# Wider 0/1 comparisons and long-lived PSUM pools in a three-layer graph network on one core

## The chip, the cores and the metric

The kernel runs on one core of a Trainium2 chip. The metric is the time of one execution on the device, in microseconds (us). The core has five engines that run side by side: TensorE (PE, matrix products), VectorE (DVE), ScalarE (ACT), GpSimd (POOL) and SyncE (SP, which issues transfers). Products land in PSUM, which has eight banks; everything else is kept in SBUF.

## The reference

There are 2500 nodes with 256 features each and 80000 edges, sorted by their end node. The features are normalized and rectified, three graph layers follow, and a last product with residual makes the output:

```
m = concat([x[dst], x[src] - x[dst]]) @ W + b     # one row for each edge
s = segment_sum(m, dst);  cnt = segment_sum(1, dst)
h' = relu(s / max(cnt, 1))                        # three times, W0 b0, W1 b1, W2 b2
out = x + concat([h, h1, h2, h3]) @ Wf + bf       # h = max(layernorm(x), 0)
```

## The kernel before

The work on edges is done with a matrix A of counts: A[source, end] is how many edges run from one node to the other. A layer is then a product of A with the node features times a weight, plus each node's own part. A has 20 tiles of 128 source rows. Its columns, the end nodes, are cut into 417 stretches of 6 end nodes; 84 stretches are a group of 504 columns, and there are five groups, the last with 81 stretches.

**How A is built.** For each stretch the at most 256 edges that end in it are fetched (two indirect transfers by POOL for each block of 128 stretches, names `ed` and `es`) and turned into two small keys for each edge: the source's place within its tile (`key_m`), and the source's tile together with the end node's place within the stretch (`key_n`). `compare(b)` takes four stretches (a *window*, number b, of 105; 21 for each group) and makes 0/1 matrices on VectorE by comparing the keys with a ramp: `one_m` (4 x 2 x 128 columns) and `one_n` (4 x 120 and 4 x 80 columns). These are three instructions, `is_equal` on bf16. `counts(b)` multiplies one by the other on PE (eight products into one PSUM bank), and `take_counts(b, a)` copies the counts on ACT into `a`, the group's part of A. The 0/1 tiles have `AHEAD` = 4 buffers, and `compare` is called four windows ahead of `counts`.

**The head.** For the first group all this stands in one order written out by hand, in which each letter is a step with its index: B is `compare`, C is `counts`, E is `take_counts`; N normalizes two node tiles (on POOL from the third pair on), T transposes them on PE, R rectifies them, Z and F are products with weights (into `pz` banks), H and L split Z's result into a high and a low part (`zh` on ACT, `zl` on DVE); "sc" makes the scales of N on DVE; "ge" issues the two indirect transfers of a block of stretches, "ka" and "kb" compute key parts on DVE, "km" one on ACT, "kt" transposes the parts on PE. Each engine keeps the order in which its instructions are written. A part of that order, in the words of the string:

```
C2 B3 k21 Z9 k11 N8 L6 B4 E2 L5 C3 B5 C4 T8 E3 E4 C5 V9 R8 E5 ge3 ka2 H9 sc2 Z7 H7 F8 G7 B6 N3 N2 ka3 km2 T2 R2 km3
kb2 C6 T3 kb3 B7 L7 kt2 Z2 B8 B9 L9 E6 C7 k22 k12 kt3 H2 N4 E7 B10 k13 k23 Z8 L2 C8 T4 C9 E8
```

**Layer 0.** While PE multiplies group g of A with `zh` and `zl` (function `layer`, line 843), the next group is built between the products (`build`, line 811): in turns of three windows, `counts` of three, `take_counts` of three, then `compare` of the three windows four further on. Each group is also written to DRAM (`a_dram`), from where layers 1 and 2 read it.

**PSUM.** In layer 0, `ps_left` (four banks) holds the sums of the layer, `ps_right` (four banks) the counts. After layer 0 both pools are closed and two new ones opened: `ps_six` for the node products and the sums of pairs of groups, `ps_two` for the group without a partner (class `Alone`), which sums over the whole first half of a layer. `bank()` takes from `ps_six`; `any_bank()`, for the 14 sums of a layer's second half, takes six, then two from `ps_two`, and so on.

**Layers 1 and 2.** First the node features are multiplied with the weights in three rounded parts (class `Nodes`, ten pairs of tiles, two banks each); two pairs behind runs the lone group's product. Then come the two pairs of groups, seven sums each (class `Stream`), and after layer 2 the last product with `Wf`, ten pairs of tiles.

Of the kernel before, what the change touches and what calls it, by code (L numbers as in the profile page):

```python
# [8 lines left out]
F32 = mybir.dt.float32  # L9
# [3 lines left out]
PSUM = bass.MemoryType.PSUM  # L13
# [255 lines left out]
BF16 = mybir.dt.bfloat16  # L269
# [44 lines left out]
def by_windows(ctx: ExitStack, tc: tile.TileContext, x, src, dst, Ws, bs, Wf, bf, out, missing):  # L314
# [3 lines left out]
    P = 128  # L318
# [6 lines left out]
    DC = D // P  # L325
    R = E // P
    W = 6
    CH = 2
# [7 lines left out]
    NB = NT * W  # L336
    N1 = NT * (W - SKIP)
    BW = 4
    TURN = 3
    REP = 2  # L340
    AHEAD = 4
# [23 lines left out]
    hot = first_layer.enter_context(tc.tile_pool(name="hot", bufs=2))  # L365
# [6 lines left out]
    def bank():  # L372
        return ps[-1].tile([P, 512], F32, name="bank")
# [66 lines left out]
    def load_wb(l, queue=SP):  # L440
        raws[l] = wpool.tile([P, DC, 2, D], F32, name="wbf", bufs=1)
        ws[l] = wpool.tile([P, DC, D], F32, name="wt"), raws[l][:, :, 0, :]
        queue.dma_start(ws[l][1], Ws[l][D:2 * D, :].rearrange("(c p) d -> p c d", p=P))

    def load_wt(l, queue=SP):
        queue.dma_start(ws[l][0], Ws[l][0:D, :].rearrange("(c p) d -> p c d", p=P))

    def load_wf(l, queue=SP):
        if l == L:
            raws[l] = wpool.tile([P, DC, 2, D], F32, name="wbf", bufs=1)  # L450
        wfs[l] = raws[l][:, :, 1, :]
        queue.dma_start(wfs[l], Wf[l * D:(l + 1) * D, :].rearrange("(c p) d -> p c d", p=P))
# [22 lines left out]
    def load_b(l, queue=SP):  # L475
        queue.dma_start(brow[PAD:PAD + 1, l % 2, :], bs[l].rearrange("(o d) -> o d", o=1))
# [71 lines left out]
    def find_next():  # L548

        ahead.append(warmed(bank()))  # L550
        PEo.matmul(ahead[0][:, 0:1], shift[:, 1:], first, start=True, stop=True)
# [212 lines left out]
    def group_of(g):  # L764
        return sum(GWS[:g]) * W, GWS[g] * W
# [8 lines left out]
    windows = [(g, s, min(BW, GWS[g] - s)) for g in range(NG) for s in range(0, GWS[g], BW)]  # L774
    ones_of = {}

    def compare(b):
        if b >= len(windows):
            return
        g, s, nb = windows[b]  # L780
        w0 = sum(GWS[:g]) + s
        one_m = hot.tile([P, BW * CH, P], BF16, name="one_m", bufs=AHEAD)
        one_n = hot.tile([P, BW, NB + N1], BF16, name="one_n", bufs=AHEAD)
        for one, iota, keys_ in (
                (one_m[:, :nb * CH, :], iota_m, key_m[:, w0:w0 + nb, :, :].rearrange("p w j r -> p (w j) r")),
                (one_n[:, :nb, :NB], iota_n, key_n[:, w0:w0 + nb, 0, :]),
                (one_n[:, :nb, NB:], iota_n[:, NB - N1:], key_n[:, w0:w0 + nb, 1, :])):
            to = one.rearrange("p k (m r) -> p k m r", r=REP)
            DVEo.tensor_tensor(
                to, iota.rearrange("p (m r) -> p m r", r=REP).unsqueeze(1).to_broadcast(list(to.shape)),  # L790
                keys_.unsqueeze(2).to_broadcast(list(to.shape)), op=OP.is_equal)
        ones_of[b] = one_m, one_n

    counted = {}

    def counts(b):
        _, s, nb = windows[b]
        one_m, one_n = ones_of.pop(b)
        pb = counted[b] = bank()
        for w in range(nb):  # L800
            PEo.matmul(pb[:, w * NB:(w + 1) * NB], one_m[:, w * CH, :], one_n[:, w, :NB], start=True, stop=False)
            PEo.matmul(pb[:, (w + 1) * NB - N1:(w + 1) * NB], one_m[:, w * CH + 1, :], one_n[:, w, NB:],
                       start=False, stop=True)
# [108 lines left out]
    banks_of = ctx.enter_context(ExitStack())  # L912
    ps_left = banks_of.enter_context(tc.tile_pool(name="ps_left", bufs=4, space=PSUM))
    head[0].close()
    ps_right = banks_of.enter_context(tc.tile_pool(name="ps_right", bufs=4, space=PSUM))
# [26 lines left out]
    def flat(l):  # L942
        return raws[l].rearrange("p c t d -> p c (t d)") if l < L else wfs[l]

    class Split:

        def __init__(self, q, parts):
            h = hT[:, :, 2 * q * P:(2 * q + 2) * P]
            high, low, across = self.parts = [p.rearrange("p (c n) -> p c n", c=DC) for p in parts]
            ACTo.activation(high, h, AF.Copy, scale=DOWN)  # L950
            DVEo.tensor_sub(low, h, high.bitcast(F32))
            DVEo.scalar_tensor_tensor(across, low.bitcast(F32), -E12, high.bitcast(F32), op0=OP.mult, op1=OP.add)
            splits[q] = self
# [77 lines left out]
        extra = chain(degrees(g + 2) if g + 2 < WG else ())  # L1031
    first_layer.close()

    banks_of.close()
    ps_six = ctx.enter_context(tc.tile_pool(name="ps_six", bufs=6, space=PSUM))
    ps_two = ctx.enter_context(tc.tile_pool(name="ps_two", bufs=2, space=PSUM))
    turn_of = [0]

    def bank():
        return ps_six.tile([P, 512], F32, name="bank")  # L1040

    def any_bank():
        turn_of[0] += 1
        return (ps_six if (turn_of[0] - 1) % 8 < 6 else ps_two).tile([P, 512], F32, name="bank")

    tmps = ctx.enter_context(tc.tile_pool(name="tmps", bufs=6))
    stage = ctx.enter_context(tc.tile_pool(name="stage", bufs=4))
# [14 lines left out]
    def combine(to, x):  # L1062
        DVEo.tensor_sub(to[:, M3:S5 + 1, :], x[:, 1::2, :], x[:, 0:2, :])
        DVEo.tensor_sub(to[:, S2, :], to[:, M3, :], x[:, 3, :])
        DVEo.tensor_add(to[:, M4, :], to[:, S2, :], x[:, 2, :])
# [139 lines left out]
    class Alone:  # L1205

        def __init__(self, l, order):
            self.l, self.order = l, order
            self.c0, self.n = group_of(alone)
            self.to = [ps_two.tile([P, 512], F32, name="bank")[:, :self.n] for _ in range(DC)]  # L1210
            self.blocks = {}

        def make(self, p):
# [25 lines left out]
    def load_alone(k, order):  # L1239
        c = order[2 * k] // 2  # L1240
        st = stage.tile([P, 8 * GS], BF16, name="staged").rearrange("p (t n) -> p t n", n=GS)[:, :4, :]
        SPo.dma_start(st, a_dram[alone][:, 4 * c:4 * c + 4, :])
        loaded[k] = st
# [45 lines left out]
    def split(q):  # L1289
        tile_ = stage.tile([P, 4 * GS], F32R, name="staged")  # L1290
        Split(q, [tile_[:, k * 2 * D:(k + 1) * 2 * D] for k in range(3)])

    for l in range(1, L):
        order = orders[l]
        lone = Alone(l, order)
        if l == 1:
            load_alone(0, order)
            split(order[2])
        pending = []
        stream = Stream(l)  # L1300
        for i in range(Q + LAG):
            if 0 < i <= Q:
                lone.make(i - 1)
            if i < Q:
                q = order[i]
                n = Nodes(l, q)
                n.multiply(splits.pop(q), coming[0])
                if i + AHEAD_H < Q and i % 2 == 1:
                    load_alone((i + 1) // 2, order)
                n.parts()  # L1310
                n.combine()
                if i + AHEAD_H < Q and order[i + AHEAD_H] not in splits:
                    split(order[i + AHEAD_H])
                pending.append(n)
            if i and pending:
                pending.pop(0).sums()
            if 0 < i <= DC:
                lone.own(i - 1, 0)
            if i >= LAG:
                lone.multiply(i - LAG)  # L1320
            if i == Q - 1:
                load_alone(Q // 2 - 1, order)
                stream.load(3)
        stream.make(2)
        lone.end()
        turn_of[0] = 0
        if l + 1 < L:
            load_b(l + 1, SPo)
            load_wb(l + 1, SPo)
            load_wt(l + 1, SPo)  # L1330
        load_wf(l + 1, SPo)
        after = orders[l + 1]

        def tick(n):
            if n == 3:
                combine(wsum, ws[l][0].rearrange("p c (o n) -> p (c o) n", o=2))
            if n == 40 and l + 1 < L:
                DVEo.tensor_sub(ws[l + 1][0], ws[l + 1][0], ws[l + 1][1])
            if n in (49, 56):
                split(after[(n - 49) // 7])  # L1340
            if n == 63 and l + 1 < L:
                load_alone(0, after)
            if n in ((65,) if l + 1 < L else (63, 65)):
                split(after[2 + (65 - n) // 2])
            if n == 64:
                raw = flat(l + 1)
                coming[:] = [Forms(raw, [raw[:, c, :] if l + 1 < L else raws[L][:, c, 0, :] for c in range(DC)])]
                coming[0].high()
                coming[0].low()
            if n == 66:  # L1350
                coming[0].across()
            if n == 67:
                coming[0].last()

        stream.run(tick)

    order = orders[L]
    for i, q in enumerate(order):
# [9 lines left out]
        for k in range(2):  # L1368
            t = 2 * q + k
            add_to_acc(t, po[k])  # L1370
            n = P if t < NT - 1 else LAST
# [42 lines left out]
```

## Time and profile before

| | us |
|---|---|
| median of 3 runs (lowest to highest) | 480.16 (479.96 to 481.01) |
| the profiled execution, its whole time | 480.26 |
| its span, first to last instruction | 478.5 |
| PE busy | 468.4 |
| DVE busy | 386.2 |
| ACT busy | 302.5 |
| POOL busy | 43.1 |
| first product of layer 0 starts | 62.07 |
| last ACT work of layer 0 ends | 206.54 |
| final products under way | 458.8 |

The granted clock of TensorE was 0.996 of full speed. Busy time is what the profiler records for an engine's own instructions; neighbouring instructions of one engine can overlap in the records, so that busy times are read together with the distance from one start to the next. All operations are recorded by one helper at line 282, so that groups are told apart by their tile names and shapes and not by their lines. A few matmul records are missing from the trace.

### The profile page before, as it was taken

Reading aid. Unit: us, or ns where it says so; the run is one execution under the profiler, and the core shown is the slowest. Engines: PE = TensorE matmul, PEld = TensorE weight load, DVE = VectorE, ACT = ScalarE, POOL = GpSimd, SP = SyncE. Lnnn points to the kernel's source line nnn. Section 1 sums busy time; section 2 is a strip of 40 time slices with the busy share of each in tenths; the row PEclk is TensorE's granted clock in tenths of the full one; section 3 lists DMA queues with packets and bytes.
Section 4 is the critical chain, followed back from the end, with each engine's and each line's share of the span. In section 5 each row is a group of like instructions: output and inputs, shape, how many; then the busy total and the mean of one; then the engine's idle time right before and its main releaser. Section 6 shows DMA issues by size and latency. Waiting matters only on the chain.

```text
span 478.5 us, 7510 instructions
## 1 busy us (share of the span) xinstructions
PE 468.4 (98%) x2728; PEld 367.8 (77%) x2728; DVE 386.2 (81%) x836; ACT 302.5 (63%) x528; POOL 43.1 (9%) x66
## 2 busy tenths in 40 slices
PE   8999999999999999999999999999999999999994
PEld 4888888777877778868887877876788788688693
DVE  8999988988899884649987847877899687569785
ACT  5776577664654335067778866874787797497530
POOL 3683015200100001000000000000000000000000
PEclk9999999999999999999999999999999999999998
DMA  8310078990550905521258641110213955220033
GB/s 284 112 54 1 2 158 160 194 210 8 108 110 2 208 9 107 112 88 49 80 194 306 216 173 25 63 43 1 86 44 92 359 176 175 86 88 0 1 106 116
DMA packets 21847, 52.75 MB, mean 110 GB/s; under 512 B 1977, under 2 KB 12170, under 8 KB 21770
## 3 DMA queue, kind: packets, MB, share of 16 engines
q1 hardware_dynamic: 14730, 34.31, 21.2%
q0 software_dynamic: 5856, 16.51, 18.1%
q10 hardware_dynamic: 1216, 1.37, 0.9%
q8 instruction: 23, 0.38, 0.3%
q14 instruction: 22, 0.18, 0.1%
HBM read 36.72 MB, written 16.10 MB: 110 GB/s over the span
## 4 chain that ended last, share of the span: by engine, by line
PE 90%; DVE 4%; POOL 3%; ACT 1%; issue 1%; DVEq 0%; POOLq 0%; ACTq 0%
PE bank L282 87%; PE pz L282 3%; POOL acc L282 2%; DVE acc L282 1%; DVE staged L282 1%; POOL ed L282 1%; ACT junk L282 1%; POOL es L282 1%; DVE st L282 0%; DVE one_m L282 0%; ACT hT L282 0%; PE turned L282 0%; DVE zl L282 0%; DVE one_n L282 0%; DVE mv L282 0%
## 5 line engine op out<-in xcount | busy, mean ns | idle before, releaser
L282 ACT CAST block<-staged 128x1008 fp32r<-128x1008 bf16 x120 | 117.9, 1032 | 16.7 <-DVE staged L282 6.3
L282 ACT CAST a<-bank 128x480 fp32r<-128x480 f32 (+1 forms) x105 | 52.9, 566 | 60.2 <-PE bank L282 60.2
L282 PE MATMUL bank<-a,zh 128*128 128x504 f32 (+1 forms) x200 | 84.3, 422 | 0.0
L282 PE MATMUL bank<-block,zh 128*128 128x504 f32 (+1 forms) x200 | 83.7, 419 | 0.0
L282 DVE TENSOR_TENSOR one_m<-iota_m,key_m 128x1024 bf16<-128x1024 bf16 (+1 forms) x105 | 72.1, 686 | 14.1 <-PE bank L282 14.0
L282 PE MATMUL bank<-a,zl 128*128 128x504 f32 (+1 forms) x200 | 77.9, 389 | 0.0
L282 PE MATMUL bank<-block,zl 128*128 128x504 f32 (+1 forms) x200 | 77.3, 387 | 0.0
L282 PE MATMUL bank<-block,sh 128*128 128x504 f32 x160 | 69.0, 431 | 0.0
L282 DVE TENSOR_TENSOR one_n<-iota_n,key_n 128x480 bf16<-128x480 bf16 (+1 forms) x210 | 66.9, 360 | 0.0
L282 PE MATMUL bank<-block,staged 128*128 128x512 f32 (+1 forms) x312 | 66.5, 364 | 0.3 <-DVE staged L282 0.3
L282 PE MATMUL bank<-block,sl 128*128 128x504 f32 x160 | 62.6, 391 | 0.0
L282 PEld LDWEIGHTS bank<-block,staged 128*128 128x128 f32 x312 | 52.5, 188 | 10.8 <-DVE staged L282 0.5
L282 DVE TENSOR_TENSOR block<-staged 128x1008 fp32r<-128x1008 bf16 x40 | 47.0, 1205 | 5.2 <-PE bank L282 3.9
L282 PEld LDWEIGHTS <-one_m 128*128 128x128 bf16 x834 | 39.3, 98 | 10.4 <-issue 3.2
L282 PEld LDWEIGHTS bank<-a,zh 128*128 128x128 f32 x200 | 37.8, 189 | 10.7 <-issue 2.6
L282 PEld LDWEIGHTS bank<-block,zh 128*128 128x128 f32 x200 | 37.6, 188 | 10.8 <-issue 2.5
L282 PEld LDWEIGHTS bank<-block,zl 128*128 128x128 f32 x200 | 37.6, 188 | 10.6 <-issue 3.2
L282 PE MATMUL bank<-one_n,one_m 128*128 128x120 bf16 x834 | 44.9, 208 | 0.3 <-DVE one_n L282 0.2
L282 PEld LDWEIGHTS bank<-a,zl 128*128 128x128 f32 x200 | 37.7, 189 | 9.0 <-issue 2.6
L282 DVE TENSOR_TENSOR staged<-staged 128x1008 bf16<-128x1008 bf16 x40 | 27.2, 679 | 17.5 <-ACT block L282 17.1
L282 PE MATMUL pz<-wbf,hT 128*128 128x256 f32 x160 | 38.4, 385 | 0.1
L282 PEld LDWEIGHTS bank<-block,sh 128*128 128x128 f32 x160 | 30.1, 188 | 10.4 <-issue 3.5
(154 smaller groups left out, 597.3 us busy)
## 6 DMA issues: line engine op xcount, KB each, us to landing
staged<-a_dram SPq DMA_DIRECT2D x52, 504.0 KB, 4.0
a_dram<-a POOLq DMA_DIRECT2D x20, 630.0 KB, 9.0
out_dram<-acc SPq DMA_DIRECT2D x17, 128.0 KB, 1.8
acc<-in_x_dram POOLq DMA_DIRECT2D x3, 640.0 KB, 12.3
wbf<-in_L_gnn_Wf_dram SPq DMA_DIRECT2D x4, 256.0 KB, 7.2
acc<-in_x_dram SPq DMA_DIRECT2D x1, 896.0 KB, 9.5
acc<-in_x_dram ACTq DMA_DIRECT2D x1, 768.0 KB, 7.0
wbf<-in_L_gnn_W_dram SPq DMA_DIRECT2D x3, 256.0 KB
```

Source lines behind the costliest of these rows:

```text
L282: return self.tc.keep_in_program_order(call(*args, **kwargs))
```

## The change

The first edit lets `compare(b)` make the 0/1 matrices of two windows, b and b+1, in the same three instructions with twice the elements, if both are of the same group and b is not 0; the call for the second window then returns at once. The tiles are twice as large and have three buffers and not four. The calls stay where they were, in the hand order and in `build`.

The second edit keeps `ps_left` and `ps_right` open after layer 0. `bank()` now takes four banks from `ps_right`, then two from `ps_left`, in a ring of six; `any_bank()` takes four and four, in a ring of eight; the lone group takes its two banks from `ps_left`. Each ring has a counter of its own, and only that of `any_bank()` is set back at the end of a first half.

```diff
     def compare(b):
-        if b >= len(windows):
+        if b >= len(windows) or b in ones_of:
             return
         g, s, nb = windows[b]
         w0 = sum(GWS[:g]) + s
-        one_m = hot.tile([P, BW * CH, P], BF16, name="one_m", bufs=AHEAD)
-        one_n = hot.tile([P, BW, NB + N1], BF16, name="one_n", bufs=AHEAD)
+        two = b > 0 and b + 1 < len(windows) and windows[b + 1][0] == g
+        nb += windows[b + 1][2] if two else 0
+        one_m = hot.tile([P, 2 * BW * CH, P], BF16, name="one_m", bufs=3)
+        one_n = hot.tile([P, 2 * BW, NB + N1], BF16, name="one_n", bufs=3)
...
         ones_of[b] = one_m, one_n
+        if two:
+            ones_of[b + 1] = one_m[:, BW * CH:, :], one_n[:, BW:, :]
...
-        one_m, one_n = ones_of.pop(b)
+        one_m, one_n = ones_of[b]
...
-    banks_of.close()
-    ps_six = ctx.enter_context(tc.tile_pool(name="ps_six", bufs=6, space=PSUM))
-    ps_two = ctx.enter_context(tc.tile_pool(name="ps_two", bufs=2, space=PSUM))
-    turn_of = [0]
+    turn_of = [0, 0]
+
+    def next_bank(i, n):
+        turn_of[i] += 1
+        return (ps_right if (turn_of[i] - 1) % n < 4 else ps_left).tile([P, 512], F32, name="bank")
 
     def bank():
-        return ps_six.tile([P, 512], F32, name="bank")
+        return next_bank(0, 6)
 
     def any_bank():
-        turn_of[0] += 1
-        return (ps_six if (turn_of[0] - 1) % 8 < 6 else ps_two).tile([P, 512], F32, name="bank")
+        return next_bank(1, 8)
...
-            self.to = [ps_two.tile([P, 512], F32, name="bank")[:, :self.n] for _ in range(DC)]
+            self.to = [ps_left.tile([P, 512], F32, name="bank")[:, :self.n] for _ in range(DC)]
...
-        turn_of[0] = 0
+        turn_of[1] = 0
```

## The prediction

> **What bounds the kernel now.** I read the page's busy shares first, then the chain that ended last in order of time, then the stretches of the timeline where the two edits lie. First the page's engine row, then the pieces of the chain at the end of the first layer:
>
> ```profile
> PE 468.4 (98%) x2728; PEld 367.8 (77%) x2728; DVE 386.2 (81%) x836; ACT 302.5 (63%) x528; POOL 43.1 (9%) x66
> ```
>
> ```profile
> 62.42 143.51 PE bank L282 x1170
> 205.93 0.02 issue
> 205.96 0.58 ACT hT L282
> 206.54 0.04 issue
> 206.58 257.35 PE bank L282 x1088
> ```
>
> TensorE is the chain: from 62.42 to 463.94 us it leaves PE once, for ACT at 205.96. VectorE is at 81% and on the chain for 4% only, so time taken off VectorE counts only where TensorE waits for it. Before 62 us the chain does wander: through DVE, then POOL from 23.23 to 37.99, then PE, with DVE comparisons from 45.68 to 47.84. So there are two places to cost: the head (20 to 62 us) and the seam at 206 us.
>
> **Part 1: comparisons of eight stretches.** Windows pair up as (1,2), (3,4) and so on; each of the five groups has 21, so window 0 and the last of groups 1 to 4 stay single. That is 50 pairs, and 105 x 3 comparisons become 55 x 3: 150 VectorE instructions less, the elements unchanged. Groups by form, then the timeline inside layer 0:
>
> ```profile
> L282 DVE TENSOR_TENSOR one_m<-iota_m,key_m 128x1024 bf16<-128x1024 bf16 x104 | 71.8, 690 | 14.1 <-PE bank L282 14.0
> ...
> L282 DVE TENSOR_TENSOR one_n<-iota_n,key_n 128x480 bf16<-128x480 bf16 x104 | 41.7, 401 | 0.0
> ...
> L282 DVE TENSOR_TENSOR one_n<-iota_n,key_n 128x320 bf16<-128x320 bf16 x104 | 33.5, 322 | 0.0
> ```
>
> ```profile
> 115.16 0.69 DVE L282 TENSOR_TENSOR one_m<-iota_m,key_m 128x1024 bf16<-128x1024 bf16 x1
> ...
> 115.76 0.64 DVE L282 TENSOR_TENSOR one_n<-iota_n,key_n 128x480 bf16<-128x480 bf16 x2
> ...
> 116.32 0.68 DVE L282 TENSOR_TENSOR one_m<-iota_m,key_m 128x1024 bf16<-128x1024 bf16 x1
> ...
> 117.26 1.08 PEld L282 LDWEIGHTS <-one_m 128*128 128x128 bf16 x24 [0.27 <-DVE one_m L282]
> ```
>
> From the three means, an element costs (690-322)/704 = 0.523 ns and an instruction about 155 ns on top. The Trainium skill, "VectorE: DVE Perf Modes", section on the fixed extra latency per instruction, says the same (measured fixed term about 150 cycles; 1224 ns for a 2048-element bf16 tensor_tensor), and that would free 150 x 0.155 = 23 us. But starts count, not busy times: a window's three take 116.32-115.16 = 1.16 us from start to start, and 1824 elements x 0.523 = 0.954, so an instruction really costs (1.16-0.954)/3 = 0.07 us. The pair takes 2.32-0.21 = 2.11 us and VectorE is freed of 150 x 0.07 = 10.5 us. The trace's spacing decides.
>
> In layer 0 (62 to 183 us) even that is worth nothing: the row at 117.26 loads windows whose comparisons were done by 116.4 (the second) and 117.56 (the third, first loaded 16 loads later, at about 117.95). Its 0.27 is no stall; the matmul before began at 117.03, the next at 117.27, the normal spacing of 0.23. The pair runs one window further ahead with buffers for six, not four, so the cover grows. If it were gone, each turn's 1.2 us of loads would be exposed; nothing moves it there.
>
> In the head PE's stalls, as spacing above the normal of its form, are few: 0.56 us at 33 us (window 5), 0.63 before 38.03, 0.15 at 45.2 (window 10), 0.37 at 48 (window 12), 0.17 at 53.3 (window 16). Two of their rows, and between them the VectorE row that step (c) turns on:
>
> ```profile
> 33.07 0.69 PE L282 MATMUL bank<-one_n,one_m 128*128 128x120 bf16 x8 [0.23 <-DVE one_n L282]
> ...
> 36.05 0.33 DVE L282 TENSOR_SCALAR lo_i<-es 128x256 int32<-128x256 int32 x1 [0.23 <-DMA es<-longer,start_i]
> ...
> 38.03 0.44 PE L282 MATMUL turned<-shift,acc 128*128 128x128 f32 x2 [0.25 <-POOL acc L282]
> ```
>
> The hand order keeps its names; the call for the second window of a pair now does nothing, so its work moves up past what stood between.
> (a) Window 5 now waits for 5 and 6 together: +0.95 (2.11-1.16), less 0.21 each for pairs (1,2) and (3,4): stall +0.5. Queued behind it on DVE: the scale `sc2`, which POOL's normalizing (row at 34.76 below) waits for.
> (b) That normalizing then meets no comparison (window 6 stood there): 1.32 falls to about 0.55, so although it starts 0.5 late, the 0.63 stall at 38.03 shrinks by about 0.5. PE is even.
> (c) The last gather (`es`) is POOL's, and DVE stands at 36.05 for its landing; key parts and pair (7,8) queue behind it, and PE's key transposes and window 7 behind those. What delays POOL's earlier work delays this. POOL's rows:
>
> ```profile
> 15.68 0.55 POOL L282 TENSOR_SCALAR acc<-acc,rs,off 128x256 f32<-128x256 f32 x1 [2.04 <-DVE off L282]
> ...
> 24.05 1.36 POOL L282 TENSOR_SCALAR acc<-acc,rs,off 128x256 f32<-128x256 f32 x1
> ...
> 28.10 1.46 POOL L282 TENSOR_SCALAR acc<-acc,rs,off 128x256 f32<-128x256 f32 x1
> ...
> 34.76 1.32 POOL L282 TENSOR_SCALAR acc<-acc,rs,off 128x256 f32<-128x256 f32 x1 [1.23 <-DVE off L282]
> ```
>
> Alone 0.55 us; beside comparisons 1.32 to 1.46, that is, 0.8 to 0.9 of waiting, as long as the DVE instruction in progress and the next two. The skill speaks against this change here: "SBUF — State Buffer", section "Who interferes with whom", says a VectorE instruction with two SBUF inputs and a GpSimd one that reads SBUF share a port under a lock held for a whole instruction, and infers that descriptor writing for DMAs is spared. By the page a wait grows by one longer instruction, 1.22-0.69 = 0.53: with two normalizings (24.05, 28.10) ahead of the gather, 1.1 us. By the trace it grows by a whole triple, 0.95: 1.9 us, and more if gathers wait too (the two at 30.32 and 32.09 last 1.46 and 1.44, the others 0.96 to 1.23). I take 1.4 for the gather's delay. Worked along the order: key parts of group 3 from 37.45 not 36.05, pair (7,8) from about 40.2 to 42.4, window 7 multiplied at 42.4 where it was 41.3: PE about +1.0, which is the delay less 0.4 that the shorter comparisons give back.
> (d) After that only DVE's pace matters: seven pairs save 1.5 us up to window 20, so the stalls at windows 10, 12 and 16 (0.69) mostly go: -0.5.
> Sum of the head: +0.5-0.5+1.0-0.5 = +0.5 us. Bounds: with no gather delay (a) +0.3, (b) -0.6, (d) -0.7, so -1.0; with four POOL operations each waiting a triple longer (3.8 us in all), (c) is +3.4 and the head +2.9.
>
> **Part 2: banks kept open.** Today the first matmul of layer 1 takes a bank of a new pool laid over the first layer's, and waits for its last reader:
>
> ```profile
> 204.13 1.79 PE L282 MATMUL bank<-hT,wt 128*128 128x486 f32 x4
> ...
> 205.96 0.58 ACT L282 ACTIVATE hT<-bank 128x486 f32<-128x486 f32 x1 [0.24 <-PE bank L282]
> ...
> 206.58 2.58 PE L282 MATMUL bank<-block 128*128 128x512 f32 x10 [0.67 <-ACT hT L282]
> ```
>
> The last old matmul starts at 205.34 and its spacing is 0.41, so PE could go on at 205.75; it goes on at 206.58: 0.83 us. After the change the bank comes from `ps_right`, whose last readers (`share`, `some`) were done by 186.3 us, and its inputs (`block`) by 193.9: -0.83. The next limit, the third node pair's split (ACT 206.43, DVE done by 208.50), is wanted at 211.3, 2.8 us later. From there PE runs 257 us without a stall, so the lead lasts to the end; there the DVE tail moves with PE. The order 4 right, 2 left is still a ring of six; the lone group holds the other two left. In layer 2 its first own product must wait for the previous layer's last readers, done at 332.3 and wanted at 337.1: nothing.
>
> No DMA is added or moved on SP's, ACT's or POOL's queue. The larger comparison buffers (7.3 KB a partition) displace others and add no wait on the path.
>
> **Sum.** -0.83+0.5 = -0.33 on a profiled execution of 480.26 us (span 478.5 plus 1.76 around it), which lies 0.10 above the median 480.16. Prediction: 479.8. A difference under 0.2%, 0.96 us, can hardly be told from no change here.
>
> **Rivals.** *Faster:* POOL is not held up, and head and seam both gain: -0.83-1.0, 478.3. For it: the stalls at windows 10 to 16 are VectorE's alone. Against: three of POOL's rows show the lock. 24%. *Slower:* POOL's place in the head decides. By (c) the head costs the gather's delay less 0.9; from 2.7 us of delay it costs 1.8 and eats the seam's gain and the 0.2% too; at 3.8 us it is +2.9, so 482.3. For it: the two long gathers. Against: much of POOL's work meets short dependent DVE operations. 13%. *The seam's gain fails:* PE finds another wait at 206; head alone, 480.7. Against: bank and inputs are ready 11 us before. 6%. That fewer comparisons are merged than said is excluded: the pairs follow from the window list.
>
> **Numbers.** The main case has 57%, its own range 479.2 to 480.4. Faster takes 24% and a small tail of the main case, 0.28; slower 0.15; the rest 0.57. With 8 in 10 inside, 478.3 to 481.2.
>
> **What would show it.** Right: one_m of 2048 elements at about 1.22 us, pairs 2.11 apart; layer 1's first matmul about 0.4 after the last of layer 0, no ACT wait before it; window 7's stall new, those of 10 and 12 gone; the landing of the last `es` after 37 us. Wrong: layer 0 starting earlier than 61.5 or later than 63.5 us, where 62.07 is now.

## The result, and the profile after

| | before | after |
|---|---|---|
| median, us (lowest to highest, runs) | 480.04 (479.24 to 481.8, 22) | 478.97 (478.3 to 480.08, 22) |
| ratio, 95% interval | | 0.9975, 0.9966 to 0.9983 |
| profiled execution, whole time | 480.26 | 478.77 |
| its span | 478.5 | 476.9 |
| layer 0's first product starts | 62.07 | 61.89 |
| layer 0's last product starts | 205.35 | 205.11 |
| layer 1's second product starts | 206.92 | 205.75 |

The changed kernel is 1.07 us faster by the medians, a quarter of a per cent. The interval takes in 0.998, the bound that the forecast had set between "faster" and "no difference to be told". The forecast was 479.8: the time is 0.8 below it, inside the range that was to hold in 8 cases of 10 (478.3 to 481.2), and 0.2 below the main case's own (479.2 to 480.4). First the page: the engine row, and the group of the wide comparison.

```profile
PE 467.6 (98%) x2728; PEld 367.8 (77%) x2728; DVE 374.3 (78%) x686; ACT 302.5 (63%) x528; POOL 41.8 (9%) x66
...
L282 DVE TENSOR_TENSOR one_m<-iota_m,key_m 128x2048 bf16<-128x2048 bf16 (+2 forms) x55 | 64.3, 1169 | 21.3 <-PE bank L282 21.3
```

VectorE has 150 instructions and 11.9 us of busy time less, and that is ten times what the kernel gained. The chain that ended last says why (start, duration, what):

```profile
31.06 2.01 POOL ed L282
33.07 0.30 issue
33.37 3.40 DMA es<-longer,start_i
...
39.13 0.43 DVE kn L282
39.55 1.13 DVE one_m L282
40.69 0.98 DVE one_n L282 x2
41.67 0.04 issue
41.71 0.93 PE bank L282 x11
...
62.24 400.53 PE bank L282 x2258
```

The last line is one piece of 400 us. Before, PE's piece broke at 205.96 for ACT; now nothing but PE lies on the chain from 62.24 to 462.77. The end of that stretch has moved from 463.94 by 1.17 us, which is just what layer 1's second product moved by, so the lead of the seam and the head lasts to the end. Ahead of it a new piece has come into the head: the gather, the key parts, and the wide comparison at 39.55, which window 7 waits for.

**The seam at 206 us.** The timeline there (start, duration, engine; a row may cover several instructions in a line):

```profile
204.90 0.58 ACT L282 ACTIVATE hT<-bank 128x486 f32<-128x486 f32 x1 [13.56 <-PE bank L282]
...
205.14 4.18 PE L282 MATMUL bank<-block 128*128 128x512 f32 x16
...
205.72 0.58 ACT L282 ACTIVATE hT<-bank 128x486 f32<-128x486 f32 x1 [0.24 <-PE bank L282]
```

ACT reads layer 0's last sum from 205.72 to 206.30, and PE no longer cares: it is in layer 1 by then. From layer 0's last product to layer 1's second (the record of the first one overlaps the product ahead of it) it was 206.92 - 205.35 = 1.57 us and is 205.75 - 205.11 = 0.64: a gain of 0.93.

**The head.** POOL's rows of after that answer to those of before, from the timeline:

```profile
24.08 2.31 POOL L282 TENSOR_SCALAR acc<-acc,rs,off 128x256 f32<-128x256 f32 x1
...
27.95 1.82 POOL L282 DMA_INDIRECT es<-in_src_dram,start_i  x1 [0.30 <-issue]
29.80 1.10 POOL L282 TENSOR_SCALAR acc<-acc,rs,off 128x256 f32<-128x256 f32 x2
31.06 2.01 POOL L282 DMA_INDIRECT ed<-longer,start_i  x1 [0.16 <-issue]
33.37 0.97 POOL L282 DMA_INDIRECT es<-longer,start_i  x1 [0.30 <-issue]
34.70 3.39 POOL L282 TENSOR_SCALAR acc<-acc,rs,off 128x256 f32<-128x256 f32 x6 [0.36 <-DVE off L282]
```

The normalizing at 24.08 took 1.36 before. The three gathers took 0.97, 1.46 and 1.44: two are longer now, the last is shorter. The normalizings at 29.80 and 34.70 are shorter too. What follows from them on PE and VectorE:

```profile
36.86 0.31 DVE L282 TENSOR_SCALAR lo_i<-es 128x256 int32<-128x256 int32 x1 [2.26 <-DMA es<-longer,start_i]
37.10 0.57 DVE L282 TENSOR_SCALAR away<-ed,below 128x256 bf16<-128x256 int32 x1
37.70 0.53 DVE L282 SCALAR_TENSOR_TENSOR away<-away 128x128 bf16<-128x128 bf16 x1
...
39.47 1.22 DVE L282 TENSOR_TENSOR one_m<-iota_m,key_m 128x2048 bf16<-128x2048 bf16 x1
```

```profile
38.95 0.44 PE L282 MATMUL bank<-shift,kn 128*128 128x128 f32 x2 [0.24 <-DVE kn L282]
...
41.31 0.23 PE L282 MATMUL bank<-one_n,one_m 128*128 128x120 bf16 x1 [0.20 <-DVE one_n L282]
41.71 0.46 PE L282 MATMUL bank<-one_n,one_m 128*128 128x80 bf16 x7 [0.17 <-DVE one_n L282]
```

The key parts start at 36.86 and not at 36.05, and PE stalls where it did not before: 0.41 us at 38.95 for `kn`, then 0.37 and 0.34 in window 7, 1.1 in all (spacing beyond the normal one of the form). In return the stall of 0.63 before 38.03 is gone, and of the 0.69 in windows 10, 12 and 16 only 0.20 at 47.78 is left. Layer 0 begins 0.18 us earlier.

So the profile's 1.6 us of shorter span are: head 0.18, layer 0 itself 0.06, seam 0.93, and 0.41 in the tail, where the time from the start of the last VectorE instruction to the end of the span, while the output is written, was 6.19 us and is 5.78. The tail is not the change's: in the profiles of this study it lay between 5.6 and 7.2 us whatever the kernel. Layer 0 took 205.35 - 62.07 = 143.28 and 205.11 - 61.89 = 143.22, from its first product to its last.

### The profile page after: what moved, and what is told of

Read it like the earlier page. It is cut to its first block, busy times and chain, and to the rows that moved or that the text cites. A ratio compares the mean times of both kernels' runs of the same rounds, so it can differ in the third digit from the quotient of the medians.

```text
span 476.9 us, 7315 instructions
## 1 busy us (share of the span) xinstructions
PE 467.6 (98%) x2728; PEld 367.8 (77%) x2728; DVE 374.3 (78%) x686; ACT 302.5 (63%) x528; POOL 41.8 (9%) x66
## 3 DMA queue, kind: packets, MB, share of 16 engines
q10 hardware_dynamic: 1216, 1.37, 0.9%
## 4 chain that ended last, share of the span: by engine, by line
PE 90%; DVE 5%; POOL 2%; ACT 1%; DMA 1%; issue 1%; DVEq 0%; ACTq 0%
PE bank L282 87%; PE pz L282 3%; DVE acc L282 1%; POOL acc L282 1%; DVE staged L282 1%; DMA es<-longer,start_i 1%; POOL ed L282 1%; ACT junk L282 1%; DVE st L282 0%; POOL es L282 0%; DVE one_m L282 0%; DVE away L282 0%; DVE kn L282 0%; DVE zl L282 0%; DVE one_n L282 0%
## 5 line engine op out<-in xcount | busy, mean ns | idle before, releaser
L282 DVE TENSOR_TENSOR one_m<-iota_m,key_m 128x2048 bf16<-128x2048 bf16 (+2 forms) x55 | 64.3, 1169 | 21.3 <-PE bank L282 21.3
L282 DVE TENSOR_TENSOR one_n<-iota_n,key_n 128x960 bf16<-128x960 bf16 (+2 forms) x110 | 55.5, 546 | 0.0
L282 PEld LDWEIGHTS <-one_m 128*128 128x128 bf16 x834 | 39.1, 98 | 10.7 <-issue 7.2
L282 PEld LDWEIGHTS bank<-block,zh 128*128 128x128 f32 x200 | 37.6, 188 | 10.8 <-issue 2.5
L282 PEld LDWEIGHTS bank<-block,zl 128*128 128x128 f32 x200 | 37.6, 188 | 10.6 <-issue 3.2
```

The source lines that it names most:

```text
L282: return self.tc.keep_in_program_order(call(*args, **kwargs))
```

## The experiments

Theory at the start: the gain is the seam's, because the bank of layer 1's first product no longer belongs to a pool laid over the closed ones; VectorE's freed time reaches PE nowhere, since in the head it is paid back by POOL, which waits longer beside wider comparisons. Rivals: the comparisons gain by themselves; or the seam's wait came from one particular bank.

To compare heads between profiles I use, beside the start of layer 0, the *head's length*: from a `pz` product that starts between 20.5 and 21.1 us in every kernel (the second after a gap of 1.5 us) to layer 0's first product. Kernels whose head is that of before (before, e1, e3, e5) have 41.46, 40.80, 40.99 and 41.10: mean 41.09, a spread of 0.3 to 0.4 to each side. The three with the change's head (after, e2, e9) have 41.28, 41.42 and 41.05: mean 41.25. Heads of one order thus differ by up to 0.66 us from profile to profile, and of the four of before's order the profile of before itself is the longest.

The runs were made in three sets, each with runs of the kernel before beside it; ratios are to those. In every profile the distance from layer 0's last product to layer 1's second is 1.57 or 1.58 us with the pools closed (before, e2, e3) and 0.64 with them kept.

| kernel | median us (runs) | ratio to before of its set, 95% | layer 0 starts | head's length |
|---|---|---|---|---|
| after | 478.97 (22) | 0.9975, 0.9966 to 0.9983 | 61.89 | 41.28 |
| *first set, before 479.68 (59)* | | | | |
| e1: pools alone | 478.83 (22) | 0.9982, 0.9975 to 0.9989 | 61.75 | 40.80 |
| e2: comparisons alone | 479.88 (13) | 1.0002, 0.9994 to 1.0010 | 62.14 | 41.42 |
| e3: pools closed, other banks | 479.74 (13) | 1.0001, 0.9993 to 1.0009 | 61.83 | 40.99 |
| e4: after, pair (7,8) earlier | 478.58 (21) | 0.9977, 0.9970 to 0.9983 | 61.78 | 40.82 |
| *second set, before 479.92 (22)* | | | | |
| e5: pairs only after the head | 478.85 (11) | 0.9984, 0.9975 to 0.9993 | 61.80 | 41.10 |
| e6: windows 1 and 2 single | 478.55 (6) | 0.9968, 0.9955 to 0.9980 | 61.83 | 41.19 |
| e7: e4, node pair 2 on ACT | 477.84 (5) | 0.9956, 0.9942 to 0.9969 | 60.65 | 40.08 |
| e8: e1, node pair 2 on ACT | 478.75 (11) | 0.9977, 0.9968 to 0.9986 | 61.31 | 40.55 |
| *third set, before 480.04 (29)* | | | | |
| e9: after, again | 478.86 (11) | 0.9978, 0.9969 to 0.9987 | 62.10 | 41.05 |
| e10: after, node pair 2 on ACT | 478.63 (12) | 0.9968, 0.9958 to 0.9978 | 61.36 | 40.66 |
| e11: e7 again | 477.74 (7) | 0.9962, 0.9947 to 0.9977 | 60.44 | 39.82 |
| e12: e8 again | 478.52 (11) | 0.9975, 0.9966 to 0.9983 | 61.55 | 40.90 |

### e1 and e2: each edit alone

e1 keeps `compare` of before and takes the pools of the change; e2 the reverse. Against the changed kernel, cut to the core:

```diff
e1
-        if b >= len(windows) or b in ones_of:
+        if b >= len(windows):
...
-        one_m = hot.tile([P, 2 * BW * CH, P], BF16, name="one_m", bufs=3)
+        one_m = hot.tile([P, BW * CH, P], BF16, name="one_m", bufs=AHEAD)
e2
+    banks_of.close()
+    ps_six = ctx.enter_context(tc.tile_pool(name="ps_six", bufs=6, space=PSUM))
+    ps_two = ctx.enter_context(tc.tile_pool(name="ps_two", bufs=2, space=PSUM))
```

> The pools kept open alone, comparisons of four stretches as before. Theory (the seam's gain and the head's gain add up): first product of layer 1 0.41 us after the last of layer 0 starts and no ACT wait before it, time 0.85 to 0.95 us below before (ratio about 0.9981), the head unchanged (layer 0 starts at 62.1 us). Rival (the whole gain is VectorE's relief, the seam's 0.83 is given back later): within 0.2 us of before.

> The comparisons of eight stretches alone, pools closed and opened as before. Theory: the head gains about 0.2 us (layer 0 starts at 61.9), the ACT wait of 0.67 us before layer 1's first product is back, time 0.1 to 0.3 us below before. Rival (VectorE's 10.5 us are worth something beyond the head): 0.8 us or more below before.

Pools alone gave 0.9982, which is the 0.85 us expected; comparisons alone 1.0002, which cannot be told from nothing; the gain of 0.1 to 0.3 us that I had expected did not come. The timelines at the seam, e1 first, then e2:

```profile
205.06 3.29 PE L282 MATMUL bank<-block 128*128 128x512 f32 x12
...
205.64 0.58 ACT L282 ACTIVATE hT<-bank 128x486 f32<-128x486 f32 x1 [0.24 <-PE bank L282]
```

```profile
205.97 0.58 ACT L282 ACTIVATE hT<-bank 128x486 f32<-128x486 f32 x1 [0.24 <-PE bank L282]
...
206.60 1.66 PE L282 MATMUL bank<-block 128*128 128x512 f32 x6 [0.67 <-ACT hT L282]
```

With the old pools PE waits for ACT's last read, with the kept pools it is 0.6 us into layer 1 when that read starts. The gain goes with the second edit.

e1 also shows that before's head does not always stand where the profile of before stood. PE in e1:

```profile
37.64 0.44 PE L282 MATMUL turned<-shift,acc 128*128 128x128 f32 x2 [0.26 <-POOL acc L282]
38.46 0.44 PE L282 MATMUL turned<-shift,acc 128*128 128x128 f32 x2 [0.38 <-POOL acc L282]
```

These are stalls of 0.43 and 0.55 us for POOL's normalizing, where before had 0.22 and 0.41, and windows 10, 12 and 16 have none. e3 and e5 look like e1.

### e3: closed pools, but other banks

Before, the two new pools lay so that the first products of layer 1 took banks that had held layer 0's last sums. e3 is the kernel before with the two pools opened in the other order, so that those products land in banks that the last sums never touched. In the built programs the last sums lie in banks 0 and 3; the first product of layer 1 goes to bank 0 before, and to bank 2 in e3.

```diff
     banks_of.close()
+    ps_two = ctx.enter_context(tc.tile_pool(name="ps_two", bufs=2, space=PSUM))
     ps_six = ctx.enter_context(tc.tile_pool(name="ps_six", bufs=6, space=PSUM))
-    ps_two = ctx.enter_context(tc.tile_pool(name="ps_two", bufs=2, space=PSUM))
```

> The kernel before with the two new pools opened in the other order, so that layer 1's first products go to two banks that the last group's sums did not use. Theory (a new pool waits until every tile of the closed one is released, whichever bank): the wait for ACT before layer 1's first product stays, time within 0.2 us of before. Rival (only the shared bank makes it wait): the wait goes, time 0.8 us below before.

The timeline of e3 at the seam:

```profile
205.73 0.58 ACT L282 ACTIVATE hT<-bank 128x486 f32<-128x486 f32 x1 [0.24 <-PE bank L282]
...
206.36 1.89 PE L282 MATMUL bank<-block 128*128 128x512 f32 x7 [0.67 <-ACT hT L282]
```

The wait is the same to 0.01 us, and the time is that of before (1.0001). It is not the bank that PE waited for but the release of the pool: here the first tile of a pool laid over closed ones waits for their last reader, though that one reads another bank. The profile of before agrees: bank 0's own last reader there was the ACT row at 205.14, done by 205.72, and the product waited for the second, which reads bank 3, until 206.54. The wait is one that the program carries: the first product is made to wait for ACT's last read.

### e4: the pair for window 7 ahead of the key parts

On the changed kernel, `B7` moves in the hand order from behind the key parts of block 3 to before them, so that the late gather no longer holds up the comparison. POOL's two normalizings there, `N3` and `N2`, change places as well, so that the pair that is transposed first comes first.

```diff
-... Z7 H7 F8 G7 B6 N3 N2 ka3 km2 T2 R2 km3
-    kb2 C6 T3 kb3 B7 L7 kt2 ...
+... Z7 H7 F8 G7 B6 B7 N2 N3 ka3 km2 T2 R2 km3
+    kb2 C6 T3 kb3 L7 kt2 ...
```

> The changed kernel with windows 7 and 8 compared straight after the scales of the normalizing, before VectorE waits for the last gather (36.9 us), and POOL normalizing the pair that is transposed first before the other. Theory (window 7's stall of 0.70 us at 41.3 comes from the comparisons queued behind the gather's landing): that stall goes; POOL's first normalizing at 34.7 waits for three comparisons and ends near 37.0 instead of 35.3, so up to 0.3 us of stall before the transposes at 37.6; layer 0 starts 0.4 to 0.7 us earlier than in the changed kernel, time 1.4 to 1.8 us below before. Rival (PE is held by something else there, or by POOL's wait): layer 0 starts no earlier than 61.8, time 1.0 us below before or less.

It measured 0.9977, 1.1 us, with layer 0 at 61.78: short of the theory's 1.4 us, and at the rival's bounds (1.0 us, 61.8). Window 7 does not stall any more, but the timeline shows what came instead; VectorE's pair, POOL, and PE:

```profile
34.52 1.22 DVE L282 TENSOR_TENSOR one_m<-iota_m,key_m 128x2048 bf16<-128x2048 bf16 x1
35.66 1.05 DVE L282 TENSOR_TENSOR one_n<-iota_n,key_n 128x960 bf16<-128x960 bf16 x2
```

```profile
34.71 2.27 POOL L282 TENSOR_SCALAR acc<-acc,rs,off 128x256 f32<-128x256 f32 x1 [0.37 <-DVE off L282]
```

```profile
37.80 0.44 PE L282 MATMUL turned<-shift,acc 128*128 128x128 f32 x2 [0.34 <-POOL acc L282]
...
39.31 0.44 PE L282 MATMUL turned<-shift,acc 128*128 128x128 f32 x2 [0.38 <-POOL acc L282]
```

POOL's normalizing starts just behind the wide comparison and ends 0.27 us behind the pair: 34.71 + 2.27 = 36.98, the pair at 36.71. In after it took 0.56 at this place. PE waits for it twice, 0.50 and 0.55 us.

### e5: pairs only after the head

```diff
-        two = b > 0 and b + 1 < len(windows) and windows[b + 1][0] == g
+        two = b > 20 and b + 1 < len(windows) and windows[b + 1][0] == g
```

> The changed kernel with single windows up to number 20 and pairs only from 21 on, that is in layer 0. Theory (VectorE's time in layer 0 is worth nothing to TensorE): VectorE is busy some 9 us less than in the kernel before, and the time is that of the pools alone, 0.7 to 1.0 us below before. Rival (the relief in layer 0 counts, and the head gives it back): 1.3 us or more below before.

Only the head's windows are single again; the larger tiles and their three buffers stay. The page's engine row:

```profile
PE 466.7 (98%) x2728; PEld 367.3 (77%) x2728; DVE 377.3 (79%) x716; ACT 302.3 (63%) x528; POOL 43.0 (9%) x66
```

Pools alone (e1) had 836 VectorE instructions and 385.6 us. The ratios are 0.9984 and 0.9982, and layer 0 takes 143.22 and 143.28 us: 8 us less of VectorE are worth 0.06 us there, for the comparisons have cover.

### e6: windows 1 and 2 single

As e5 with `b > 2`. It takes the wide comparison away from beside the normalizing at 24 us.

> The changed kernel with windows 1 and 2 single again and all other pairs kept. Theory (a POOL instruction waits for the VectorE instruction in progress and the next two, so its length follows theirs): the normalizing at 24.1 us takes 1.36 us again, not 2.31; the gathers behind it start about 0.9 earlier, the last gather lands near 36.0, the stalls at 38.95 and 41.3 shrink from 1.1 to 0.3 or less; layer 0 starts up to 0.7 us earlier than in the changed kernel. Rival (POOL's length is its own jitter): it stays above 2 us or varies, and the landing stays near 36.8.

The theory held on POOL and fell on the gain: the normalizing at 24.2 took 1.37 us again, but the one at 28.27 took 2.26, since it now met a pair; the last gather landed at 36.69 and not near 36.0. And window 5 came later. PE in e6:

```profile
33.83 0.23 PE L282 MATMUL bank<-one_n,one_m 128*128 128x120 bf16 x1 [0.96 <-DVE one_n L282]
34.23 0.46 PE L282 MATMUL bank<-one_n,one_m 128*128 128x80 bf16 x7 [0.17 <-DVE one_n L282]
...
39.56 0.38 PE L282 MATMUL bank<-shift,kn 128*128 128x128 f32 x2
```

The stalls at 39 and 41 us are gone (0.08 is left), but 1.1 + 0.3 us in window 5, which had 0.5, stand for them. The head's length, 41.19, is that of after. The median, from 6 runs, is lower than after's, but the intervals of the two ratios overlap by most of after's, so it shows no gain.

### e7 and e8: less POOL in the head

e7 is e4 with node pair 2 normalized on ACT, at a place where ACT has room. e8 does the same to e1: comparisons of four, and `B7` behind the key parts, where before has it. So e8 differs from e7 in two things, the width of the comparisons and the place of `B7`. The cut shows e7 against e4:

```diff
-            if q >= 2:
+            if q > 2:
...
-... H9 sc2 Z7 H7 F8 G7 B6 B7 N2 N3 ka3 ...
+... H9 sc2 N2 Z7 H7 F8 G7 B6 B7 N3 ka3 ...
```

> The kernel with windows 7 and 8 compared early, and node pair 2 normalized on ACT (two instructions of 0.59 us) and not on POOL. Theory (with window 7's stall gone, what TensorE waits for at 37.8 is POOL held up by the longer comparisons): the stalls of 0.50 and 0.55 us at 37.8 and 39.3 go, layer 0 starts near 60.9, time 1.8 to 2.2 us below before. Rival (VectorE or ACT is late next, stalls reappear at windows 9 to 16): layer 0 starts at 61.5 or later, time 1.0 to 1.3 us below before.

> Pools kept open, comparisons of four stretches, node pair 2 normalized on ACT. Theory (without pairs VectorE bounds the head once POOL no longer does): the stalls before the transposes at 37.6 and 38.5 go, but TensorE stands at windows 10 to 16 for 0.7 us or more; layer 0 starts 0.2 to 0.5 us before 61.75, time 1.0 to 1.4 us below before. Rival (VectorE has slack there): layer 0 starts near 60.8, as early as with pairs.

e7 came out as expected: layer 0 starts at 60.65, 2.1 us below before in time. In e8 POOL's stalls are gone as well, but VectorE's are back, 0.17, 0.20, 0.17 and 0.17 us between 44 and 53, and the time is 0.9 us above e7.

### e9 to e12: the same side by side

e7 had only five runs, and its set had none of the changed kernel, so the changed kernel (e9), e7 (e11) and e8 (e12) were run in one set, with one new kernel: e10 is the changed kernel with node pair 2 on ACT and `B7` left behind the key parts. It differs from e12 in the width of the comparisons alone.

```diff
-            if q >= 2:
+            if q > 2:
...
-... H9 sc2 Z7 H7 F8 G7 B6 N3 N2 ka3 ...
+... H9 sc2 N2 Z7 H7 F8 G7 B6 N3 ka3 ...
```

> The changed kernel as it is, beside the three others on one chip. Ratio to before expected 0.9975 (0.9966 to 0.9983 earlier); layer 0's first product between 61.7 and 62.0 us.

> The changed kernel with node pair 2 normalized on ACT, but pair (7,8) of comparisons left behind the key parts. Theory: the stalls of the changed kernel at 38.95 (0.4) and 41.3 (0.7) come from the gather's landing and from the comparisons queued behind its key parts, which this edit leaves where they are; so they stay, layer 0 starts within 0.3 us of the changed kernel's, and the ratio is 0.9975 within 0.0008. Rival: POOL's load alone holds PE; then the stalls go, layer 0 starts near 60.7, and the ratio is that of both edits together, 0.9956.

> Both edits together (pair (7,8) ahead of the key parts, node pair 2 normalized on ACT) on the changed kernel, on the same chip as it. Theory: 1.0 to 1.2 us below the changed kernel, ratio to before 0.9956 against 0.9975, with intervals that do not meet. Rival: the earlier difference, between two chips, was partly theirs, and it is under 0.5 us here.

> Node pair 2 on ACT, pools kept open, comparisons four stretches at a time, on the same chip. Theory: 0.5 to 1 us above the version with eight at a time and both edits, ratio 0.9972 to 0.998: the wider comparisons are worth that once POOL does not hold PE. Rival: they are worth nothing anywhere, and the two are equal within 0.3 us.

e9 repeats after: 0.9978, with layer 0 at 62.10, a little outside the stretch that I had given. e11 repeats e7: 1.12 us below e9 by the medians, layer 0 1.66 us earlier. Its interval still overlaps e9's, from 0.9969 to 0.9977, against what I expected; but the two pairs of runs agree (1.13 and 1.12 us), so this is the fastest version of the study, 2.1 to 2.3 us below before. The chain of e11 has PE in one piece from 60.80 on:

```profile
60.80 400.53 PE bank L282 x2258
```

e12 is 0.78 us above e11, e8 was 0.91 above e7. With intervals that overlap in the third set and in the second (0.9968 and 0.9969) just meet, that is likely and not shown by the times alone; the traces say the same (head's length 40.90 and 40.55 against 39.82 and 40.08). But it is not the worth of the wider comparisons, as their place differs too. With the place left alone, e12 and e10, the times are 478.52 with four and 478.63 with eight, and the heads 40.90 and 40.66: POOL's relief by itself did not make the wider comparisons worth anything that these runs can tell. Nor did the wider comparisons at the earlier place without that relief (e4 is 0.25 us below e1, with intervals that overlap). The 0.8 us came with all of it together. Comparisons of four with the earlier place were not run, so how the 0.8 us divide between width and place stays open.

e10 lies between theory and rival: window 7 still stalls (0.26 and 0.34), as the theory said, but the stall at 38.95 is gone and layer 0 starts 0.5 us earlier than in after, which it did not say. PE in e10, then VectorE, which shows why:

```profile
40.78 0.23 PE L282 MATMUL bank<-one_n,one_m 128*128 128x120 bf16 x1
41.18 0.46 PE L282 MATMUL bank<-one_n,one_m 128*128 128x80 bf16 x7 [0.17 <-DVE one_n L282]
```

```profile
36.81 0.29 DVE L282 TENSOR_SCALAR lo_i<-es 128x256 int32<-128x256 int32 x1 [2.18 <-DMA es<-longer,start_i]
37.02 0.35 DVE L282 TENSOR_SCALAR away<-ed,below 128x256 bf16<-128x256 int32 x1
37.41 0.29 DVE L282 SCALAR_TENSOR_TENSOR away<-away 128x128 bf16<-128x128 bf16 x1
...
38.94 1.22 DVE L282 TENSOR_TENSOR one_m<-iota_m,key_m 128x2048 bf16<-128x2048 bf16 x1
```

The gather lands as late as in after (36.81 and 36.86), but from there to the comparison it is 2.13 us and not 2.61. In after POOL normalizes until 38.09, beside the key parts; in e10 it is done by 36.90. The two `away` take 0.35 and 0.29 there, 0.57 and 0.53 in after. In the thirteen other profiles POOL still normalizes somewhere in this stretch, and it is 2.52 to 2.94 us long in all of them. So 0.4 of the 1.1 us of new stalls, the one at `kn`, was POOL slowing VectorE, not the gather's delay alone. POOL slowed VectorE there in before too, whose stretch was 2.94 us; it cost PE nothing, as PE came to these products only at 39.1.

## Why the prediction was right and where its sum was wrong

The seam was right, mechanism and size: -0.83 predicted, -0.93 measured (the 0.10 more is the second product's wider spacing after the old wait), and the lead lasts to the end as said. e3 adds what the text had only assumed, that the wait belongs to the pool laid over the old ones and not to one bank.

In the head the price of an instruction was right. Two pairs in a row in after:

```profile
45.55 1.21 DVE L282 TENSOR_TENSOR one_m<-iota_m,key_m 128x2048 bf16<-128x2048 bf16 x1
...
47.65 1.22 DVE L282 TENSOR_TENSOR one_m<-iota_m,key_m 128x2048 bf16<-128x2048 bf16 x1
```

The pair's three take 2.10 us from start to start, as the sum said (2.11), and not the 2.3 - 0.46 = 1.9 that the fixed latency of the Trainium skill's "VectorE: DVE Perf Modes" would make. The wide comparison takes the 1.22 us forecast; the 1224 ns that the prediction set beside it stands on that page in another section, the table of perf modes. That next to none of the saving counts in layer 0 was right (e5: 0.06 us). The step that failed is the head's sum of +0.5, by its terms:

- **(a), window 5, +0.5: wrong.** It stalls for 0.51 us in all, and did for 0.56. The pair (5,6) costs what was said, but it starts at 31.01, where window 5 alone had started at 32.02: the work ahead of it gave back 1.0 us and not the 0.42 that I had allowed. 0.6 of it was there before pair (3,4) (27.70 for 28.31), 0.4 from there to pair (5,6). The first 0.6 are mostly POOL's: in before its normalizings stretched `one_m` of windows 1 and 2 to 0.97 and 0.88 us from 0.68, in after `one_m` of the pair to 1.50 from 1.22, once and not twice, and windows 1 and 2 take 2.39 us where they had taken 2.80; the key parts behind them take 1.65 where they had taken 1.88. The sum had counted what comparisons do to POOL, and not what POOL does to comparisons.
- **(b), -0.5, and (d), -0.5: right together.** Against the profile of before, the stalls of 0.63 before 38.03 are gone, and so are those at 45.2 and 53.3; 0.2 of the 0.37 at 48 is left: -1.1. But the division was that one profile's: e1, e3 and e5, with comparisons of four in the head, have 0.98 to 0.99 us of POOL's stalls at 37.6 and 38.5 and none at windows 10 to 16, so against them it is -0.8. The normalizing at 34.70 took 0.56, as predicted.
- **(c), gather late by 1.4, PE +1.0: the delay was wrong, and the +1.0 was met by luck.** VectorE goes on behind the gather's landing 0.81 us later (36.86 for 36.05), so the landing after 37 us that was to show the forecast right did not come. A POOL operation does wait for three VectorE instructions (2.31 us beside a wide triple), and the gathers wait too, but most of it was given back: the normalizing at 29.80 met `zl` and no comparison and took 0.56 where its like had taken 1.46, and the last gather took 0.97 where it had taken 1.44. PE lost 1.1 us all the same, 0.7 in window 7 and 0.4 at `kn`, which the sum did not have; that one goes when POOL's work beside the key parts goes (e10).

Their sum was measured as -0.18 in one pair of profiles, +0.16 as the difference of the mean head's lengths, and +0.2 us (1.0002) by e2's time: nothing, within a spread of 0.3 to 0.4. Take the +0.5 away and the forecast is 480.26 - 0.83 - 0 = 479.4; from the median of the larger sample, 480.04, it is 479.2, against 478.97 measured. So the main case's sign was right, and its head was too dear by some 0.3 to 0.5 us. That is also why "faster by over 0.2%", which the median makes it, had a chance of only 0.28: seam and bound are of one size, and the head decided between the two answers. The rival that gave 478.3 was nearer in time and wrong in its reason: POOL was held up (2.31 us), and head and seam did not both gain. The slower rival's place was right (POOL in the head, gathers waiting too); the price was not.

## What to carry to other kernels

Before closing a memory pool and opening another over it, look at who reads the old one last: here the new pool's first tile waited for that reader though it used another bank, and keeping the pools open cost nothing. A larger instruction on an engine that is off the path can still cost on the path, through an engine that waits beside it (POOL here) and through what is queued behind it; count both sides, for the same edit also moves other work to places where it waits for nothing. An engine's freed time is worth what the waits on it are worth: 8 us in layer 0 gave 0.06, and in the head about 0.8 us showed only where POOL's work was cut and the pair for window 7 was moved up as well. And one profile of a head can differ by 0.66 us from another of the same order, so read a small stall in several before you count on its going away.

## What the hardware showed that was not expected

- A POOL normalizing beside a run of VectorE comparisons waits for more than the one in progress. It took 0.55 us alone, 1.36 beside a triple of comparisons of which the last two take 0.4 and 0.3 us, and 2.31 beside one of which they take 0.6 and 0.5. In the fourteen profiles, all normalizings of 1.3 us or more but one end 0.26 or 0.27 us behind the second VectorE instruction after the one in progress. In two of the kernels it shows that this is not the triple's end: at 28.10 in before and at 28.27 in e6 (1.46 and 2.26 us) the one in progress was `kn`, and POOL got in ahead of the triple's third. The one exception (39.94 in e4) waited for the next one only, as did the shorter waits of about 0.8 us. The Trainium skill, "SBUF — State Buffer", section "Who interferes with whom", has a lock held for one instruction; at 34.71 in e4 the one in progress ended at 35.74, which would make about 1.03 + 0.55 = 1.6 us, and it took 2.27. The measurements decide; why it is two more stays open.
- The gathers wait in the same way: 0.97 before and 1.82 after at one place, 1.46 and 2.01 at another, and each of the long ones ends 0.26 to 0.29 us behind the end of a comparison. That section infers that writing descriptors is spared; in these rows it is not. No run isolated a gather.
- It works in the other direction too: the key parts of block 3, seven VectorE instructions, took 2.13 us from the first to what follows in e10, where POOL had ended its normalizing, and 2.52 to 2.94 in the thirteen profiles in which it had not.
